# A two-layer bottleneck network: the last stage's held rows moved between the last tile's products, and VectorE's order written out in three places

## The chip, the cores and the metric

The kernel runs on one core of a Trainium2 chip. A core has TensorE (PE, matrix products, results in PSUM), VectorE (DVE), ScalarE (ACT), GpSimd (POOL) and SyncE (SP, which here only issues DMAs). The engines run side by side and wait for one another through semaphores. The metric is the device time of one execution in microseconds (us), as the median of several runs; fewer is better.

## The reference

Two layers in a row, each a residual bottleneck on 64 images of 1024 channels and 14 x 14 pixels, all in 32-bit floats:

```python
out = relu(bn(conv1x1(x, w1) + b1))        # 1024 -> 256 channels
out = relu(bn(conv3x3(out, w2) + b2))      # 256 -> 256
out = bn(conv1x1(out, w3) + b3)            # 256 -> 1024
x   = relu(x + softplus(residual_scale) * out)
```

`bn` takes its mean and variance over all images and pixels of the batch, so a layer's last normalization can only be applied when the statistics of all pixels are known. The change touches what follows that point in the second layer.

## The kernel before, in words

Channels lie on the 128 partitions. A *tile* t (0 to 31) is two images, PX = 392 pixels; its 1024 channels are CS = 8 *rows* of 128 x 392. The 256 channels after the second convolution stay in SBUF as `y`, in MS = 2 slots.

The statistics of the second layer's last convolution come from a Gram matrix of `y` (`gram`). VectorE transposes `y` piece by piece from a copy called `home` (L1309) into small `zt` tiles, of which there are six in a ring; TensorE multiplies each with itself into the bank `ap`. In between, TensorE makes the products of tile 0, which ACT saves as `z` (eight rows), and ENDED = 3 products of the last tile 31, which ACT saves as `held`. The closure `beside` hangs other work on given steps of that loop: four weight sums (L148), and at step `total - 4` the four sums of `y` that the first pair of tiles needs (`pair_sums`, `column_sums`, L501 to L504).

Then `final`, the last stage. The third convolution of tiles 1 to 30 is done in 15 *pairs* of tiles, with seven block products in place of eight (a Strassen-like scheme), so each pair needs four sums of `y` (L501 to L504, tiles `ct`) and sums of weights (`ws`). A *unit* (`Conv3Pair`) is one pair and two of its rows, q and q + 4; there are 60 units. A unit has seven products, p1 to p7, of 128 x 392 each, in the PSUM banks `cy`, `cx` and `cp` (two of each). Around them stand:

- ACT copies scaled banks to `cu` (after p1, p6 and p7), so that the bank can be written again;
- VectorE adds scaled banks to the rows of x (`add`, L536, after p2, p3, p4 and p5);
- GpSimd adds `cu` to the rows of x (L559 after p7, L667 after p3);
- ACT applies the last ReLU in place to three of the unit's four rows (`end`), VectorE to the fourth (L676, in `go_out`), and SP issues the unit's two stores (L679).

`stream` sets the order of the products: a unit's p3 and p4 are done within the following unit (`last`), and the first two units begin together. `stream` yields once per product; `final` counts these yields in k and hangs tile 0's rows on them. The eight rows of tile 0 are completed by `residual`: a VectorE instruction that adds the scaled `z` row to the x row (L1816), and an ACT ReLU that the caller issues later. `go_out` is called once more than two units are open. The rows 0 to 2 of tile 31 are completed from `held` in the last pair, one for each of its first three units, by `residual(...)()`. `ending` then makes the products of tile 31's rows 3 to 7 (the last in two halves), completes them and stores the tile in pieces (L1846); rows 0 and 1 are stored together.

What sets the order: all products (L167) and all ACT calls through `act` (L342) are given to their engines in the order of the program. VectorE's, GpSimd's and SP's instructions are not, unless `tc.keep_in_program_order` is called on them: then an instruction is put behind the one that was traced before it on its engine. All others the planner of the language sorts at compile time, by its own estimate of when each is ready and by their place in the program; it may bring an instruction far forward. `run(ins)` pins an instruction only while the list `pinned` has an entry. `go_out`'s L676 is always pinned, the stores never are.

The tiles of x come by DMA into six buffers; tile 31's load is issued while the pair 27 and 28 is worked on.

Of the kernel before, what the change touches and what calls it, by code (L numbers as in the profile page):

```python
# [12 lines left out]
ALU = mybir.AluOpType  # L13
# [5 lines left out]
CS = C // P  # L19
# [54 lines left out]
def bottlenecks(ctx: ExitStack, tc: tile.TileContext, x, w1s, w2s, w3s, pars, out):  # L74
# [1736 lines left out]
    def residual(xt, o, ps, aff, here=slice(0, PX)):  # L1811


        scale, shift = aff
        v = xt[:, o, here]
        nc.vector.scalar_tensor_tensor(v, ps, scale[:, o : o + 1], v, ALU.mult, ALU.add)  # L1816
        return partial(act, v, v, AF.Relu, bias=shift[:, o : o + 1])
# [13 lines left out]

    def ending(psum, xt, w3, aff):

        for o in range(CS):
            parts = 2 if o + 1 == CS else 1
            for i in range(parts):
                here = slice(i * PX // parts, (i + 1) * PX // parts)
                if o >= ENDED:
                    ps = psum.tile(PX // parts)
                    for s in range(MS):  # L1840
                        matmul(ps, w3[:, s, o, :], two(T - 1, s)[:, here], start=s == 0, stop=s == MS - 1)
                    residual(xt, o, ps, aff, here)()
                a = o - 1 if o % 2 and o + 1 < CS else o
                if o % 2 or o + 2 == CS:
                    queue = nc.scalar if o + 1 == CS and i + 1 == parts else nc.sync
                    queue.dma_start(  # L1846
                        out=out[T - 1][:, a * PX + here.start : o * PX + here.stop],
                        in_=xt[:, o, here] if a == o else xt[:, a : o + 1].rearrange("p s f -> p (s f)"),
                    )

# [4 lines left out]
    def final(psum, pool, sums_pool, xpool, xs, z, held, summed, a, w3, aff):  # L1855
# [4 lines left out]
        def pairs():  # L1860
            for t in range(1, T - 1, 2):
                ys, sums = summed.pop(0) if summed else pair_sums(sums_pool, t)
                for q in range(CS // 2):
                    units.append(Conv3Pair(psum, pool, xs[t : t + 2], q, PX, ys, sums, w3, aff, out[t : t + 2]))
                    yield units[-1]

                    while len(units) > 2:
                        units.pop(0).go_out()
                    if t == T - 3 and q < ENDED:
                        residual(xs[T - 1], q, held[:, q], aff)()  # L1870
                    if q == 1:

                        for i in range(len(xs), min(t + len(xpool), T)):
                            xs.append(load_x(xpool[i % len(xpool)], 1, i))

        relus = [residual(xs[0], o, z[:, o], aff) for o in range(HELD)]
        for k, _ in enumerate(stream(pairs(), (T // 2 - 1) * CS // 2, together=True), 1):
            if k % 2 == 0 and k // 2 <= CS - HELD:
                o = HELD + k // 2 - 1
                relus.append(residual(xs[0], o, z[:, o], aff))  # L1880
            if k % 2 == 0 and relus:
                relus.pop(0)()
                if not relus:
                    nc.gpsimd.dma_start(out=out[0], in_=xs[0].rearrange("p s f -> p (s f)"))
        for unit in units:
            unit.go_out()
        ending(psum, xs[T - 1], a, aff)

# [323 lines left out]
    for b in range(2):  # L2212
# [9 lines left out]
        with tc.tile_pool(name=f"last_{b}", bufs=1, **({"reuse_waits": "tile"} if b == 0 else {})) as one, tc.tile_pool(  # L2222
# [12 lines left out]
            with ExitStack() as scope:  # L2235
# [10 lines left out]
                with tc.tile_pool(name=f"gram_{b}", bufs=1) as pool:  # L2246
# [11 lines left out]
                    else:  # L2258
# [4 lines left out]
                        beside = {total - 14 + 2 * i: partial(next, summed) for i in range(4)}  # L2263
                        beside[total - 4] = lambda: first_sums.append(pair_sums(sums_pool, 1))
                        grams = gram(psum, pool, homes, z, own, aff, minus_c, w3, beside)
# [76 lines left out]
```

## Time and profile before

| | |
|---|---|
| median of 3 runs | 1891.18 us (1890.45 to 1892.38) |
| profiled execution | 1890.67 us |
| its span, first to last instruction | 1888.9 us |
| TensorE busy | 1867.8 us, 99% |
| VectorE busy | 1573.1 us, 83% |
| ScalarE busy | 1111.2 us, 59% |
| GpSimd busy | 742.1 us, 39% |
| first product of the last stage starts | 1592.13 us |
| last product of the last stage starts | 1882.82 us |

How to read the rows that follow. A row of the timeline reads: start in us, duration in us from the first start to the last end of the merged instructions, engine, line, operation, output<-inputs, shape, count, and in square brackets how long the engine had been idle and what ended that. Buffer numbers are left out of names: `cy` is either of two banks. One product of 128 x 392 is two matmul instructions (x2). PEld is the loading of weights, which overlaps PE; DVEq, SPq and ACTq are the engines' sequencers, which issue DMAs and wait on semaphores. Ends of matmuls are modelled, so distances between starts are used here. A row of the chain of waits reads: start, duration, what. A row of a table by stretch reads: from:to, length, busy time of each engine with its count, granted TensorE clock, share of the DMA engines, GB/s.

### The profile page before, as it was taken

To read this page: it belongs to the slowest core of one execution; us is meant where nothing else is said; L and a number is where in the kernel's file an instruction comes from. 1 tells how busy PE (TensorE), PEld (TensorE's weight loads), DVE (VectorE), ACT (ScalarE), POOL (GpSimd) and SP (SyncE) were. 2 spreads that over 40 slices of the span, in tenths; PEclk is the share of its full clock that TensorE was granted. 3 is DMA by queue.
4 is the path that set the end of the run, shared out by engine and by line. 5 is a ranking of instruction groups with operands and counts; after the bars stand their busy time and mean duration, and the time that the engine had idled before them with its cause. 6 is when DMAs were issued, how large, how long until landed. Compare 5 with 4: busy or idle time off the path is not lost. (4 is left out here: it accounts for less than half of the span.)

```text
span 1888.9 us, 28626 instructions
## 1 busy us (share of the span) xinstructions
PE 1867.8 (99%) x9728; PEld 1555.5 (82%) x9728; DVE 1573.1 (83%) x2494; ACT 1111.2 (59%) x2329; POOL 742.1 (39%) x763
## 2 busy tenths in 40 slices
PE   9999999999999999999999999999999999999998
PEld 5555557999998998899999999999999986555554
DVE  5787867999998776778788788799999986888886
ACT  2222214677777665555555555457777694666665
POOL 0111100121205655377776776311121151666665
PEclk9999999999999999999999999999999999999999
DMA  7777644797865556778788887468788465999997
GB/s 288 269 253 271 217 182 137 204 218 216 207 201 163 183 175 213 252 270 321 269 281 299 296 297 278 193 184 223 212 208 221 141 175 224 343 338 334 334 347 281
DMA packets 246609, 458.87 MB, mean 243 GB/s; under 512 B 41456, under 2 KB 212992, under 8 KB 233280
## 3 DMA queue, kind: packets, MB, share of 16 engines
q1 hardware_dynamic: 208288, 375.30, 58.8%
q0 software_dynamic: 31328, 29.18, 7.9%
q10 hardware_dynamic: 6848, 52.57, 6.9%
q8 instruction: 77, 1.26, 0.3%
q14 instruction: 68, 0.56, 0.1%
HBM read 289.44 MB, written 141.03 MB: 228 GB/s over the span
## 5 line engine op out<-in xcount | busy, mean ns | idle before, releaser
L167 PE MATMUL columns<-v,ub 128*128 128x224 f32 (+1 forms) x1536 | 303.5, 339 | 1.4 <-ACT columns L342 0.8
L342 ACT ACTIVATE x<-x,shift 128x392 f32<-128x392 f32 x453 | 260.3, 613 | 71.7 <-DVE x L536 31.4
L167 PEld LDWEIGHTS columns<-v,ub 128*128 128x128 f32 x1536 | 268.6, 188 | 8.4 <-ACT columns L342 1.5
L342 ACT ACTIVATE cu<-cy,scale 128x196 f32<-128x196 f32 (+1 forms) x360 | 175.5, 499 | 163.0 <-PE cy L167 155.5
L167 PE MATMUL ay<-at,ws 128*128 128x196 f32 (+1 forms) x760 | 191.6, 383 | 0.4 <-ACT au L342 0.2
L667 POOL TENSOR_TENSOR x<-x,cu 128x392 f32<-128x392 f32 x120 | 125.7, 1048 | 111.5 <-DVE x L536 109.4
L167 PEld LDWEIGHTS ay<-at,ws 128*128 128x128 f32 x760 | 134.8, 190 | 35.7 <-issue 0.9
L536 DVE SCALAR_TENSOR_TENSOR x<-cp,scale,x 128x196 f32<-128x196 f32 (+1 forms) x240 | 124.4, 518 | 45.6 <-PE cp L167 44.2
L342 ACT ACTIVATE au<-ay 128x196 f32<-128x196 f32 (+1 forms) x139 | 53.5, 385 | 169.8 <-PE ay L167 159.8
L167 PE MATMUL l<-diffs,ub 128*128 128x224 f32 (+1 forms) x768 | 149.7, 337 | 0.4 <-DVE diffs L803 0.3
L167 PE MATMUL m<-sums,ua 128*128 128x224 f32 (+1 forms) x752 | 146.0, 336 | 1.2 <-issue 0.6
L167 PEld LDWEIGHTS l<-diffs,ub 128*128 128x128 f32 x768 | 134.6, 189 | 1.8 <-DVE diffs L803 1.1
L167 PEld LDWEIGHTS m<-sums,ua 128*128 128x128 f32 x752 | 131.4, 189 | 2.7 <-issue 0.9
L1104 POOL DMA_DIRECT2D y<-f x24 | 32.1, 1636 | 257.5 <-DVE f L1003 257.5
L167 PE MATMUL cx<-y,w 128*128 128x196 f32 (+1 forms) x404 | 124.7, 395 | 0.0
L559 POOL TENSOR_TENSOR x<-x,cu 128x196 f32<-128x196 f32 (+1 forms) x120 | 104.3, 869 | 45.7 <-ACT cu L342 27.3
L167 PE MATMUL cy<-y,w 128*128 128x196 f32 (+1 forms) x372 | 115.6, 398 | 1.7 <-ACT y L342 0.9
L342 ACT ACTIVATE y<-y,shift,scale 128x320 f32<-128x320 f32 (+9 forms) x105 | 110.2, 1074 | 7.1 <-DVE shift L2082 6.4
L564 POOL TENSOR_TENSOR x<-x,cu 128x392 f32<-128x392 f32 x60 | 80.4, 1340 | 84.8 <-DVE x L536 82.0
L214 POOL DMA_DIRECT2D u<-y x48 | 26.0, 543 | 211.3 <-ACT y L342 210.5
L963 ACT ACTIVATE columns<-m 128x448 f32<-128x448 f32 (+1 forms) x144 | 70.8, 492 | 56.1 <-PE m L167 49.1
L1931 POOL TENSOR_SCALAR y<-y,scale 128x392 f32<-128x392 f32 x57 | 92.3, 1620 | 28.5 <-DVE scale L2283 28.5
(331 smaller groups left out, 4510.7 us busy)
## 6 DMA issues: line engine op xcount, KB each, us to landing
ub<-u SPq DMA_DIRECT2D x92, 768.0 KB, 5.5
x<-in_x SPq DMA_DIRECT2D x35, 1568.0 KB, 8.3
x<-mid SPq DMA_DIRECT2D x32, 1568.0 KB, 7.5
out<-x SPq DMA_DIRECT2D x123, 392.0 KB, 6.9
mid<-x ACTq DMA_DIRECT2D x30, 1568.0 KB, 9.1
x<-in_x SPq DMA_DIRECT2D x108, 392.0 KB, 7.8
ua<-u SPq DMA_DIRECT2D x92, 256.0 KB, 3.1
z<-kept SPq DMA_DIRECT2D x60, 392.0 KB, 2.9
```

The lines of the kernel that those rows point to most:

```text
L167: tc.keep_in_program_order(nc.tensor.matmul(*args, **kw))
L214: nc.gpsimd.dma_start(out=us[b][i][:, s, o], in_=u)
L342: tc.keep_in_program_order(nc.scalar.activation(*args, **kw))
L536: run(nc.vector.scalar_tensor_tensor(v, bank, self.scale[:, o : o + 1], v, ALU.mult, ALU.add))
L559: run(nc.gpsimd.tensor_add(self.part(1, 1), self.part(1, 1), u3))
L564: run(nc.gpsimd.tensor_add(v, v, self.u12))
L667: nc.gpsimd.tensor_add(v, v, self.u12[:, i * self.n : (i + 1) * self.n])
L963: copy(v, m, AF.Copy)
L1104: nc.gpsimd.dma_start(out=out_rows[3][:, o], in_=fa[:, o, :full], accum_op=ALU.add)
L1931: run(nc.gpsimd.tensor_scalar(z, z, scale[:, o : o + 1], None, ALU.mult))
```

## The change

Five edits in the second layer's last part.

1. `residual` issues its VectorE instruction through `run`, so it is pinned where `pinned` is set.
2. In the last pair of `final`, the three calls of `residual` on the held rows are gone, and `go_out` is called once more than one unit is open (before: two).
3. In `final`, VectorE and GpSimd instructions that go through `run` are pinned up to the 14th product. Rows 0 to 4 of tile 0 are still begun ahead of the products; rows 5, 6 and 7 are begun at k = 5, 8 and 11 (before: 2, 4 and 6).
4. `ending` is rewritten: after the product of row 3, 4 and 5 each, held row 0, 1 and 2 is completed; all of its VectorE instructions are pinned. Rows 0 and 1 are stored after row 4's product, rows 2 and 3 and rows 4 and 5 after row 5's.
5. The four sums for the first pair are pinned at step `total - 4` of the Gram loop.

```diff
@@ residual
-        nc.vector.scalar_tensor_tensor(v, ps, scale[:, o : o + 1], v, ALU.mult, ALU.add)
+        run(nc.vector.scalar_tensor_tensor(v, ps, scale[:, o : o + 1], v, ALU.mult, ALU.add))
         return partial(act, v, v, AF.Relu, bias=shift[:, o : o + 1])
@@ ending
-    def ending(psum, xt, w3, aff):
-
-        for o in range(CS):
-            parts = 2 if o + 1 == CS else 1
-            for i in range(parts):
-                here = slice(i * PX // parts, (i + 1) * PX // parts)
-                if o >= ENDED:
-                    ps = psum.tile(PX // parts)
-                    for s in range(MS):
-                        matmul(ps, w3[:, s, o, :], two(T - 1, s)[:, here], start=s == 0, stop=s == MS - 1)
-                    residual(xt, o, ps, aff, here)()
-                a = o - 1 if o % 2 and o + 1 < CS else o
-                if o % 2 or o + 2 == CS:
-                    queue = nc.scalar if o + 1 == CS and i + 1 == parts else nc.sync
-                    queue.dma_start(
-                        out=out[T - 1][:, a * PX + here.start : o * PX + here.stop],
-                        in_=xt[:, o, here] if a == o else xt[:, a : o + 1].rearrange("p s f -> p (s f)"),
-                    )
+    def ending(psum, xt, held, w3, aff):
+
+        def store(a, e, queue=nc.sync):
+            queue.dma_start(out=out[T - 1][:, a:e], in_=xt.rearrange("p s f -> p (s f)")[:, a:e])
+
+        def product(o, i=0, parts=1):
+            here = slice(i * PX // parts, (i + 1) * PX // parts)
+            ps = psum.tile(PX // parts)
+            for s in range(MS):
+                matmul(ps, w3[:, s, o, :], two(T - 1, s)[:, here], start=s == 0, stop=s == MS - 1)
+            residual(xt, o, ps, aff, here)()
+
+        pinned.append(True)
+        for o in range(ENDED, CS - 1):
+            product(o)
+            if o < 2 * ENDED:
+                residual(xt, o - ENDED, held[:, o - ENDED], aff)()
+            for a, e, by in (0, 2, 4), (2, 4, 5), (4, 6, 5), (6, 7, 6):
+                if by == o:
+                    store(a * PX, e * PX)
+        for i in range(2):
+            product(CS - 1, i, 2)
+            a = (CS - 1) * PX + i * PX // 2
+            store(a, a + PX // 2, (nc.sync, nc.scalar)[i])
+        pinned.clear()
@@ final
-                    while len(units) > 2:
+                    while len(units) > 1 + (t < T - 3):
                         units.pop(0).go_out()
-                    if t == T - 3 and q < ENDED:
-                        residual(xs[T - 1], q, held[:, q], aff)()
                     if q == 1:
 
                         for i in range(len(xs), min(t + len(xpool), T)):
                             xs.append(load_x(xpool[i % len(xpool)], 1, i))
 
+        pinned.append(True)
         relus = [residual(xs[0], o, z[:, o], aff) for o in range(HELD)]
         for k, _ in enumerate(stream(pairs(), (T // 2 - 1) * CS // 2, together=True), 1):
-            if k % 2 == 0 and k // 2 <= CS - HELD:
-                o = HELD + k // 2 - 1
+            if k in (5, 8, 11):
+                o = HELD + (k - 5) // 3
                 relus.append(residual(xs[0], o, z[:, o], aff))
+            if k == 14:
+                pinned.clear()
             if k % 2 == 0 and relus:
                 relus.pop(0)()
                 if not relus:
                     nc.gpsimd.dma_start(out=out[0], in_=xs[0].rearrange("p s f -> p (s f)"))
         for unit in units:
             unit.go_out()
-        ending(psum, xs[T - 1], a, aff)
+        ending(psum, xs[T - 1], held, a, aff)
@@ bottlenecks, beside the Gram loop
-                        beside[total - 4] = lambda: first_sums.append(pair_sums(sums_pool, 1))
+
+                        def sums_now():
+                            pinned.append(True)
+                            first_sums.append(pair_sums(sums_pool, 1))
+                            pinned.clear()
+
+                        beside[total - 4] = sums_now
```

## The prediction

> **What bounds the kernel now.** I read the page first, then the busy times by stretch of the last stage, then PE's timeline for starts that come late, then the other engines' timelines at those places.
>
> ```profile
> PE 1867.8 (99%) x9728; PEld 1555.5 (82%) x9728; DVE 1573.1 (83%) x2494; ACT 1111.2 (59%) x2329; POOL 742.1 (39%) x763
> 1621.00:1858.00 237.00, 237.00 (x712) 134.08 (x711) 198.47 (x305) 161.20 (x305) 164.20 (x153) 1.00 0.95 338
> 1858.00:1877.00 19.00, 16.27 (x49) 8.65 (x48) 12.86 (x21) 12.12 (x24) 9.99 (x10) 1.00 0.67 243
> 1877.00:1889.00 12.00, 6.65 (x25) 4.12 (x23) 5.89 (x11) 5.07 (x9) 2.24 (x3) 0.87 0.72 263
> ```
>
> TensorE is the bound: 237.00 of 237.00 us busy in the middle of the last stage, at a granted clock of 1.00. So only places where PE starts late, and what follows its last product, can give time. In the stretch up to 1877 it is 2.73 us short (19.00 - 16.27); after that the work drains into DMA.
>
> ```profile
> 1859.78 0.82 PE L167 MATMUL cy<-ct,w 128*128 128x392 f32 x2
> 1863.31 0.93 PE L167 MATMUL cy<-ct,ws 128*128 128x392 f32 x2 [2.71 <-ACT cu L342]
> 1861.18 2.02 DVE L1816 SCALAR_TENSOR_TENSOR x<-held,scale,x 128x392 f32<-128x392 f32 x3
> 1862.16 0.62 ACT L342 ACTIVATE x<-x,shift 128x392 f32<-128x392 f32 x1 [2.88 <-DVE x L1816]
> 1862.68 0.57 ACT L342 ACTIVATE cu<-cy,scale 128x392 f32<-128x392 f32 x1
> 1865.55 1.32 PE cy L167 x4
> 1872.13 1.32 PE cy L167 x4
> ```
>
> The last two rows (from the chain of waits) are 10 products apart: 0.658 us a product. The rows above show the largest stall: the three held rows' VectorE work stands together at 1861.18. ACT, whose order is fixed, has the first held row's ReLU ahead of a `cu` copy, waits 2.88 us for it, and PE needs the copy.
>
> **The change part by part.**
>
> *Held rows out of the last pair (edit 2).* The step 1859.78 to 1863.31 is 3.53, less 0.66 is 2.87; and the product that starts at 1863.31 takes 0.93 where the one before it takes 0.82, 0.10 more. Together 2.97 us. With the ReLU gone, ACT's copy has nothing to wait for but its bank. What is late next? Unit 58 instead gets a second L676 (0.9 us, by the rows of the ending below); VectorE has three held instructions fewer there (2.02 us), so it is not later than now. The ReLUs of held rows 1 and 2 also leave the pair. I take -2.97; the other end is 0, if another wait fills the place.
>
> *First products (edit 3).*
>
> ```profile
> 1591.98 4.38 DVE L1816 SCALAR_TENSOR_TENSOR x<-z,scale,x 128x392 f32<-128x392 f32 x8
> 1595.42 1.48 PE L167 MATMUL cy<-ct,ws 128*128 128x392 f32 x4
> 1596.82 0.61 DVE L536 SCALAR_TENSOR_TENSOR x<-cp,scale,x 128x392 f32<-128x392 f32 x1
> 1597.48 0.93 PE L167 MATMUL cp<-y,ws 128*128 128x392 f32 x2 [0.59 <-DVE x L536]
> 1598.02 1.01 POOL L559 TENSOR_TENSOR x<-x,cu 128x392 f32<-128x392 f32 x1
> 1596.28 1.25 ACT L342 ACTIVATE cu<-cy,scale 128x392 f32<-128x392 f32 x2
> 1599.06 2.80 ACT L342 ACTIVATE x<-x,shift 128x392 f32<-128x392 f32 x5 [1.03 <-POOL x L559]
> 1602.38 0.93 PE L167 MATMUL cy<-ct,w 128*128 128x392 f32 x2
> ```
>
> The planner has brought all eight rows of tile 0 ahead of the first adds. With 4.38/8 = 0.55 each, five pinned rows end at about 1594.7, the add from `cx` at 1595.2, row 5 at 1595.7. The `cp` add needs the product that ends where the two `cy` products (x4) start, 1595.42; it is then next in the queue and ends at about 1596.4 instead of 1597.43. PE's `cp` product can then start at 1595.42 + 1.32 = 1596.74, 0.74 earlier. But the gain does not all stay: at 1602.38 PE waits for ACT, which did five ReLUs in a row after waiting for GpSimd's L559. L559 needs the add and the later of the two `cu` copies, which ACT ends at 1597.53, so it can start at about 1597.57, 0.45 earlier, not 1.07. ACT's five ReLUs and PE's product at 1602.38 move by that. I take -0.46. Ends: -1.13, all that PE loses here (0.74 and 0.11 at 1597.48, 0.28 at 1602.38), and +0.5, below among the rivals.
>
> *The first pair's sums (edit 5).*
>
> ```profile
> 1558.98 0.55 DVE L501 TENSOR_TENSOR ct<-y 128x392 f32<-128x392 f32 x1
> 1560.88 0.55 DVE L504 TENSOR_TENSOR ct<-y,ct 128x392 f32<-128x392 f32 x1
> 1561.36 1.29 DVE L1309 STREAM_TRANSPOSE zt<-home 128x512 f32<-128x512 f32 x2
> 1564.94 3.98 DVE L1309 STREAM_TRANSPOSE zt<-home 128x512 f32<-128x512 f32 x7
> 1560.74 0.75 PE L167 MATMUL ap<-zt 128*64 128x193 f32 x8
> 1562.11 6.80 PE L167 MATMUL ap<-zt 128*64 128x193 f32 x96 [0.62 <-DVE zt L1309]
> 1575.88 2.96 PE L167 MATMUL ap<-zt 128*64 128x193 f32 x40
> 1558.70 2.18 DMA home<-y
> ```
>
> Five sums (one of them for the second pair) stand from 1558.98 to 1561.36 in front of a transpose, and PE waits for that transpose. PE's 96 matmuls take 6.80, so eight take 0.57: after 1560.74 it would go on at 1561.31, not 1562.11: 0.80 lost. Step `total - 4` puts the four sums between the eighth and ninth of the last eleven transposes, after the first four of the row of seven. The last three transposes then come 4 x 0.48 = 1.9 us later, at about 1570; PE needs them at 1575.88, some 6 us of cover. Without that cover the cost would be 1.9. The transpose needs data, though: the chain of waits names a move into `home` that ends at 1560.88. By that, only 1561.36 - 1560.88 = 0.48 can be won. But the transpose starts 0.48 after L504 did, the very spacing of the sums, so I read VectorE's queue as what held it, and take -0.80. Ends: -0.80 and 0.
>
> *The ending (edits 2 and 4), in the times of before.*
>
> ```profile
> 1867.70 0.57 SPq L1846 DMA_DIRECT2D out<-x  x1
> 1877.64 1.82 DVE L676 TENSOR_SCALAR x<-x,shift 128x392 f32<-128x392 f32 x2
> 1879.28 0.62 ACT L342 ACTIVATE x<-x,shift 128x392 f32<-128x392 f32 x1 [0.47 <-POOL x L667]
> 1878.40 0.53 SPq L679 DMA_DIRECT2D out<-x  x1
> 1884.14 0.46 ACT L342 ACTIVATE x<-x,shift 128x196 f32<-128x196 f32 x1
> GB/s 368 13 0 0 0 0 0 155 393 381 142 0 0 0 29 372 355 351 381 376 364 385 372 376 368 385 393 368 393 393 401 381 345 339 322 44 0 0 0 0
> ```
>
> PE's products are the same. VectorE now has three L676 here (the first two shown), then two, and gains three held instructions of 0.54: from 1877.64 + 1.82 = 1879.46 it runs row 3, held 0, row 4, held 1, row 5, held 2 until about 1882.7; the last three are bound by PE as now. ACT runs seven ReLUs of some 0.54 from 1879.28 + 0.62 = 1879.9, and the last one, now at 1884.14, comes about 0.1 later.
>
> DMA decides more. The rate row (0.375 us a slice, from 1874) is full from about 1879.5 to 1887.4: the store issued at 1878.40 begins to move 1.1 later, and with those behind it 7 x 392 KB (two rows of 128 x 392 floats each) go out in 7.9 us, 1.1 each at some 365 GB/s. The change moves rows 0 and 1 (392 KB) from 1867.70 into this queue, past SP's other stores, and takes one store of unit 58 out of it, to before 1876. The amount is equal. But three stores are done at 1879.5 + 3.3 = 1882.8, and rows 0 and 1 cannot go before held row 1's ReLU, about 1882.3; their data begin 1.1 later, at 1883.4. From there four times 1.1 ends at 1887.8, not 1887.4. I take +0.4. Ends: -0.2 (ACT's last store, issued at 1884.6, alone decides) and +1.1 (392 KB that find no gap).
>
> The Trainium skill (DMA: Bandwidth & Descriptors, section "Anatomy of one DMA") fits a transfer as about 2.0 us plus bytes at 436 GB/s. By that, an estimate from its figures, 392 KB would take 0.92 in the queue instead of 1.10 and this term would be near -0.2. The slices here top out near 400 GB/s and average some 365, so the trace does not agree; the sum keeps the rows.
>
> *What comes along: the second pair's sums.*
>
> ```profile
> 1606.44 0.82 PE L167 MATMUL cp<-y,ws 128*128 128x392 f32 x2
> 1608.61 1.45 DVE L502 TENSOR_TENSOR ct<-ct,y 128x392 f32<-128x392 f32 x1
> 1617.18 0.82 PE L167 MATMUL cy<-ct,w 128*128 128x392 f32 x2
> 1654.71 1.32 PE cy L167 x4
> 1841.51 1.32 PE cy L167 x4
> ```
>
> Ten pairs later in the stage take 186.80, 18.68 each, against 28 x 0.658 = 18.42: 0.26 lost per pair, at its sums. At the second pair's sums PE loses more: 15 products from 1606.44 to 1617.18 take 10.74, not 9.87: 0.87. VectorE's sum takes 1.45 there, with GpSimd behind its usual place. Engines that come 0.46 earlier may relieve part of it; the planner decides anew. I take -0.2, between -0.6 (as a later pair) and +0.6.
>
> **The sum.** -2.97 - 0.46 - 0.80 + 0.4 - 0.2 = -4.0. The profiled execution took 1890.67 (span 1888.9 and 1.8 around it), so 1886.7; the median is 0.51 above it: 1887.2.
>
> **Rivals.**
>
> ```profile
> L1816 DVE SCALAR_TENSOR_TENSOR x<-held,scale,x x3: 614/615/940, 1861.2 to 1862.6; 128x392 f32<-128x392 f32 x3
> 1860.69 1.01 POOL L667 TENSOR_TENSOR x<-x,cu 128x392 f32<-128x392 f32 x1 [0.32 <-DVE x L536]
> ```
>
> *The tail or the start takes its full price.* The tail at +1.1, or the start at +0.5: rows 6 and 7 of tile 0 now stand in the time of GpSimd's adds, and the first held row, begun at 1861.18 while an add of GpSimd ran, took 0.94 against 0.61 for the other two. If two such rows each wait out most of a 1.01 us add, `cp` adds come late and the start loses what it gained. Against it: ACT, not VectorE, is the bound there once the `cp` add is early, which leaves VectorE slack. The Trainium skill (SBUF — State Buffer, section "Who interferes with whom") says that a VectorE instruction with two SBUF inputs and a GpSimd instruction reading SBUF exclude each other, so that one waits in full. By that rule this price is due wherever the two meet; the 0.94 agrees with it. With either price: -3.0 to -3.4, about 1888.1.
>
> *More comes along.* The second pair's sums fall to the usual 0.26, and the tail finds its gap: -5.0, 1886.2. For it: later pairs show that rate with the same order of instructions.
>
> *The stall stays under another name.* ACT's order is still fixed and the two L676 of unit 58 come at its start; if PE waits there for VectorE or the planner moves the stores into SP's way, edit 2 gives nothing: -1.0, about 1890.2. Against it: 2.02 us of VectorE's work leave the same place.
>
> *Slower.* The planner re-sorts the unpinned VectorE and GpSimd work of all pairs behind the new start. If every pair's sums met GpSimd as the second pair's do, each of 13 pairs would lose 0.61 more: +7.9 - 4.0 = +3.9, 1895.1. It decides from 0.31 us a pair on. Against it: ten pairs in a row return to the same 18.68, whatever happened at 1608.
>
> **How the numbers follow.** The forecast 0.46, tail or start in full 0.22, more comes along 0.18, the stall stays 0.06, slower 0.08. 0.2% (3.8 us) is about what a measurement of this kernel can tell from no change. The forecast's own range, 1886.4 to 1888.0, straddles that bound: 0.30 over it and 0.16 within. So faster 0.48, same 0.16 + 0.22 + 0.06 = 0.44, slower 0.08. The range 1885.2 to 1889.4 holds the first three cases and leaves out the last two and some edges, about 0.2.
>
> **What would show it.** Right: no PE idle of over 0.3 us in the last pair; held instructions between L1816's of `cy` and `cx` only, spaced 0.54; the first `cp` product of the stage 0.66 after its neighbour, and ACT still the releaser of a `cy` product some 5 us on; no PE idle before the last eleven transposes, sums between the eighth and ninth; DMA nearly full over the last 8 us, its data ending 0.4 us later behind the last product than now. Wrong: a new releaser of PE in units 57 to 60, more than 18.8 us a pair, or a DMA hole over 1 us before rows 0 and 1 go out.

## The result, and the profile after

The changed kernel takes 1886.76 us (median of 11 runs, 1886.01 to 1888.36), the kernel before 1891.87 us in the same comparison (11 runs, 1890.22 to 1892.77). The ratio is 0.9975, with a 95% interval of 0.9966 to 0.9984: faster by 0.25%, just over what this kernel's measurement can tell from no change. Predicted were 1887.2 us. The profiled execution took 1886.24 us, its span is 1884.5 us, 4.4 less than the 1888.9 of before.

The page of the changed kernel (busy time of the engines), and its busy times by stretch of the last stage; the columns are those of the prediction's first fence:

```profile
PE 1867.1 (99%) x9728; PEld 1556.6 (83%) x9728; DVE 1572.8 (83%) x2494; ACT 1111.7 (59%) x2329; POOL 744.6 (40%) x763
```

```profile
1618.00:1855.00 237.00, 237.00 (x712) 134.03 (x711) 198.54 (x305) 161.26 (x305) 164.72 (x153) 1.00 0.97 341
1855.00:1871.00 16.00, 15.98 (x49) 8.84 (x49) 11.24 (x19) 11.19 (x22) 9.84 (x10) 1.00 0.79 282
1871.00:1884.50 13.50, 7.04 (x26) 4.37 (x24) 7.29 (x13) 6.43 (x12) 2.63 (x3) 0.96 0.65 238
```

TensorE bounds the stage as before. The stretch before the ending, 2.73 us short in the kernel before, is now full (15.98 of 16.00). The last row is 1.5 us longer than before's (13.50 against 12.00, partly by where it was cut), with VectorE busy for 7.29 instead of 5.89: the held rows have come there.

The places that the prediction names, in the timelines of the changed kernel, from the Gram products to the last pair:

```profile
1564.13 1.31 DVE L1309 STREAM_TRANSPOSE zt<-home 128x512 f32<-128x512 f32 x2 [0.87 <-PE ap L167]
1565.36 1.00 DVE L501 TENSOR_TENSOR ct<-y 128x392 f32<-128x392 f32 x2
...
1567.23 0.56 DVE L504 TENSOR_TENSOR ct<-y,ct 128x392 f32<-128x392 f32 x1
1567.71 1.63 DVE L1309 STREAM_TRANSPOSE zt<-home 128x512 f32<-128x512 f32 x3
...
1552.73 14.67 PE L167 MATMUL ap<-zt 128*64 128x129 f32 x212
...
1593.91 1.48 PE L167 MATMUL cy<-ct,ws 128*128 128x392 f32 x4
1595.23 0.82 PE L167 MATMUL cp<-y,ws 128*128 128x392 f32 x2
...
1600.40 0.93 PE L167 MATMUL cy<-ct,w 128*128 128x392 f32 x2
...
1597.20 2.67 ACT L342 ACTIVATE x<-x,shift 128x392 f32<-128x392 f32 x5 [0.68 <-POOL x L559]
...
1857.14 0.82 PE L167 MATMUL cy<-ct,w 128*128 128x392 f32 x2
1857.80 0.82 PE L167 MATMUL cy<-ct,ws 128*128 128x392 f32 x2
```

All sums stand behind the eighth of the last eleven transposes, and PE goes through 212 Gram matmuls without a gap. The stage's first `cp` product starts 1.32 behind the two `cy` products (x4), with no wait. ACT still has its five ReLUs in a row behind GpSimd's L559, so a wait of 0.28 us is left at the `cy` product of 1600.40. The two `cy` products that were 3.53 us apart at the held rows are 0.66 apart.

The ending: VectorE, ACT and SP by time, the DMA rate (0.41 us a slice from 1868.2), and SP's own waits over the last pair (what it waited for, us in total, times, the longest):

```profile
1872.03 1.83 DVE L676 TENSOR_SCALAR x<-x,shift 128x392 f32<-128x392 f32 x2
1873.78 0.61 DVE L1816 SCALAR_TENSOR_TENSOR x<-cy,scale,x 128x392 f32<-128x392 f32 x1
1874.31 0.61 DVE L1816 SCALAR_TENSOR_TENSOR x<-held,scale,x 128x392 f32<-128x392 f32 x1
1868.36 1.63 ACT L342 ACTIVATE x<-x,shift 128x392 f32<-128x392 f32 x3
1866.00 1.20 SPq L679 DMA_DIRECT2D out<-x  x2
1872.83 0.53 SPq L679 DMA_DIRECT2D out<-x  x1
```

```profile
GB/s 377 381 296 0 0 0 0 0 0 0 0 0 0 0 262 358 381 373 369 381 354 381 373 385 393 408 423 370 369 377 383 421 319 385 333 83 0 0 0 0
```

```profile
SPq L679 <- DVE x L676: 13.7, 4, 5.6
```

VectorE's order is as written. But SP issues nothing between 1867.2 and 1872.83, and DMA moves nothing for eleven slices. Unit 59's store of tile 30 was ready when ACT's three ReLUs ended, at 1870.0. It stands in SP's queue behind unit 59's store of tile 29, which waits for L676 at 1872.03. Then seven stores of 392 KB and the three pieces of rows 6 and 7 (392 KB together) go out in one row. In the kernel before, ACT's three ReLUs of unit 59 and SP's next store read:

```profile
1873.97 1.63 ACT L342 ACTIVATE x<-x,shift 128x392 f32<-128x392 f32 x3
1875.63 0.53 SPq L679 DMA_DIRECT2D out<-x  x1
```

There tile 30's store goes out 0.03 us behind its ReLUs, 2.77 ahead of the next one (1878.40), and is no part of the last row. That row has six stores of 392 KB and the three pieces: one store less.

**Where the time went.** Steps between the same products of PE, worked out from their start times in each profile: 18 Gram matmuls around the gap; from the stage's first product pair to the `cy` product that waits for ACT; the 15 products at the second pair's sums; ten later pairs; the two `cy` products at the held rows; from there to the last product; from its start to the span's end. The kernels of the experiments stand below.

| kernel | Gram | start | second pair | ten pairs | held rows | rest | tail |
|---|---|---|---|---|---|---|---|
| before | 2.07 | 10.26 | 10.75 | 186.80 | 3.53 | 19.52 | 6.07 |
| changed | 1.21 | 9.78 | 10.05 | 186.84 | 0.66 | 19.41 | 7.25 |
| e8_before | 2.16 | 10.25 | 10.75 | 186.83 | 3.53 | 21.21 | 6.07 |
| e8_after | 1.20 | 9.78 | 10.05 | 186.84 | 0.66 | 19.42 | 7.25 |
| e1_sums | 1.21 | 10.26 | 10.05 | 186.81 | 3.52 | 19.52 | 6.07 |
| e2_start | 2.13 | 9.77 | 10.75 | 186.81 | 3.53 | 21.02 | 6.07 |
| e3_end | 2.15 | 10.26 | 10.05 | 186.83 | 0.66 | 19.42 | 7.25 |
| e4_inplace | 2.15 | 10.26 | 10.05 | 186.81 | 3.52 | 22.30 | 6.07 |
| e4_relus | 1.95 | 10.25 | 10.04 | 186.81 | 0.66 | 20.17 | 7.12 |
| e5_swap | 1.20 | 9.78 | 10.75 | 186.81 | 0.66 | 19.41 | 6.46 |
| e6_port | 1.21 | 10.37 | 10.97 | 184.33 | 0.66 | 19.41 | 6.34 |
| e7_all | 1.20 | 10.38 | 10.87 | 184.33 | 0.66 | 20.28 | 5.30 |
| e9_best | 1.21 | 9.58 | 9.88 | 184.33 | 0.66 | 20.03 | 5.45 |
| e10_late | 1.20 | 9.59 | 9.88 | 184.33 | 0.66 | 19.42 | 5.60 |

Changed less before: -0.86 - 0.48 - 0.70 + 0.04 - 2.87 - 0.11 + 1.18 = -3.80. Another -0.58 lies ahead of every changed place (the `cy` product with which tile 0 begins starts at 1510.40, not 1510.98; over the fourteen profiles it starts between 1509.90 and 1511.73). The rest, below 0.1, lies between the steps.

### The profile page after: what moved, and what is told of

Its sections match the earlier page's. It is cut to its first block, busy times and chain, and to the rows that moved or that the text cites. A ratio compares the mean times of both kernels' runs of the same rounds, so it can differ in the third digit from the quotient of the medians.

```text
span 1884.5 us, 28626 instructions
## 1 busy us (share of the span) xinstructions
PE 1867.1 (99%) x9728; PEld 1556.6 (83%) x9728; DVE 1572.8 (83%) x2494; ACT 1111.7 (59%) x2329; POOL 744.6 (40%) x763
## 5 line engine op out<-in xcount | busy, mean ns | idle before, releaser
L559 POOL TENSOR_TENSOR x<-x,cu 128x196 f32<-128x196 f32 (+1 forms) x120 | 104.9, 874 | 46.6 <-ACT cu L342 18.6
```

The lines of the kernel that those rows point to most:

```text
L559: run(nc.gpsimd.tensor_add(self.part(1, 1), self.part(1, 1), u3))
```

## The experiments

The expectations count the tail to the last byte, some 1.1 us ahead of the span's end that the table uses: their 5.0 is the table's 6.07, their 6.10 its 7.25.

### The three places one by one

`e1_sums`, edit 5 alone:

```diff
-                        beside[total - 4] = lambda: first_sums.append(pair_sums(sums_pool, 1))
+                        def sums_now():
+                            pinned.append(True)
+                            first_sums.append(pair_sums(sums_pool, 1))
+                            pinned.clear()
...
+                        beside[total - 4] = sums_now
```

> The kernel before with edit 5 alone (the first pair's sums fixed behind the eighth of the last eleven transposes). Theory (VectorE's queue held the transpose): the row of 96 Gram products and the row of 40 join without an idle stretch, 0.80 to 0.86 us won, and nothing else in the last stage moves: 10.25 us from the stage's first product of a pair to the cy product that waits for ACT, 10.74 us over the 15 products at the second pair's sums, 3.53 us at the held rows, 5.0 us from the last product to the last byte. Rival 1 (the move into home held it): 0.48 won. Rival 2 (moving the sums is what relieved the second pair's sums, one of the five being theirs): the 10.74 falls to about 10.05 here.

Measured: 1888.34 us against 1890.93. The Gram step falls by 0.86, so VectorE's queue held the transpose. The second pair fell to 10.05 too, as the second rival had it. The next two kernels tell whether that comes from the sums.

`e2_start`, edits 1 and 3 alone (`run(...)` around `residual`'s instruction, and the loop of `final`):

```diff
+        pinned.append(True)
         relus = [residual(xs[0], o, z[:, o], aff) for o in range(HELD)]
...
-            if k % 2 == 0 and k // 2 <= CS - HELD:
-                o = HELD + k // 2 - 1
+            if k in (5, 8, 11):
+                o = HELD + (k - 5) // 3
...
+            if k == 14:
+                pinned.clear()
```

> The kernel before with edits 1 and 3 alone (VectorE's order fixed at the stage's first products). Theory: 10.25 us from the first product of the stage to the cy product that waits for ACT becomes 9.78 (0.47 won); the Gram gap of 0.80, the 3.53 at the held rows and the tail of 5.0 stay. For the second pair's sums, theory A: what is late there is set by the start, so 10.74 falls to about 10.05 with this edit alone, 1.16 won in all. Theory B: it comes from elsewhere, and 10.74 stays, 0.47 won in all.

Measured: 1891.64 us against 1890.93. The start won 0.49, and the second pair stayed at 10.75: theory B. Yet the time is no better, for 1.50 us were lost in "rest", behind a stall that this edit doesn't touch. The busy times by stretch show why; the third column from the right is the clock that PE was granted:

```profile
1859.01:1862.42 3.41, 1.06 (x4) 0.29 (x2) 2.94 (x5) 0.80 (x2) 1.84 (x2) 1.00 1.05 370
1862.42:1865.84 3.42, 3.07 (x5) 1.80 (x6) 0.29 (x2) 1.66 (x4) 0.00 (x0) 0.50 0.45 155
```

From 1862.42 on, just ahead of the end of the stall at the held rows, PE's clock was half for 3.4 us.

`e3_end`, edits 1, 2 and 4 alone (the new `ending`, and in the pairs):

```diff
-                    while len(units) > 2:
+                    while len(units) > 1 + (t < T - 3):
                         units.pop(0).go_out()
-                    if t == T - 3 and q < ENDED:
-                        residual(xs[T - 1], q, held[:, q], aff)()
```

> The kernel before with edits 1, 2 and 4 alone (held rows out of the last pair, completed in the ending). Theory: 3.53 us at the held rows becomes 0.66 to 0.7 and no other idle of over 0.3 us appears in the last pair, 2.97 won; the tail from the last product to the last byte grows from 5.0 to 6.1, because the second store of unit 59 stands in SP's queue behind its first, which waits for VectorE's L676: 1.9 us won in all. Rival for the tail (rows 0 and 1 going out late are its whole cause, 0.4): 5.4. The start (10.25) and the second pair's sums (10.74) stay.

Measured: 1888.00 us against 1890.93. The held step becomes 0.66 (2.87 less, and 0.10 more in "rest"), and the tail grows by 1.18, not by the rival's 0.4. The second pair came out at 10.05, with every instruction of every engine there in the order of before. So that 0.70 is none of the edits'.

### Two things that change from one execution to the next

Both kernels unchanged, profiled again:

> The kernel before, unchanged, profiled again. Theory (two things in its profile are a matter of the execution and not of the program: at the second pair's sums a VectorE sum and a GpSimd add become ready within 0.02 us of each other and either may win the port; after the stall at the held rows PE's granted clock either stays 1.0 or falls to 0.5 for 2 to 3 us): the 15 products at the second pair's sums take 10.74 or about 10.05 us with nothing between; the step at the held rows is 3.53 us again, with or without 1.3 to 1.6 us more behind it. Rival (they belong to the program): 10.74 again and nothing more behind the stall.

> The changed kernel, unchanged, profiled again. Theory as in the run before it: 10.05 or 10.74 us over the 15 products at the second pair's sums (10.05 in its first profile), PE's granted clock at 1.0 through the last pair since no stall is left there. Rival (the change relieves the second pair's sums): 10.05 again. The sum of the terms otherwise within 0.3 us of its first profile, from the Gram products to the last byte.

Measured: 1893.31 and 1886.46 us. The kernel before has the 10.75 again, and this time loses 1.69 us behind its stall:

```profile
1864.20:1867.40 3.20, 3.18 (x6) 1.84 (x7) 0.63 (x1) 2.12 (x4) 0.10 (x1) 0.62 0.65 224
```

Of the five profiles that have the stall of some 2.7 us, two kept a clock of 1.00 behind it (before and e1_sums) and three did not (e2_start, e4_inplace, e8_before). The clock thus belongs to the execution. In the three, the half clock lasts 3.41 us each (from 1862.42, 1862.59 and 1864.97), and PE was busy for 0.71 to 1.06 us of the 3.41 us ahead of it. The Trainium skill (TensorE: Matmul & The Clock Gate, section "What's actually happening") describes it: a monitor counts PE's activity in free-running windows of about 3.4 us, and an idle window halves the clock. The trace agrees as to the half (0.50), the length (3.41) and the chance of it. That a stall of 2.7 us, shorter than such a window, can be enough, it shows beyond the page.

The second pair is the same kind of thing. Rows of three kernels, VectorE's sum L502 and GpSimd's adds; first the kernel before, then e1_sums, then e5_swap (below):

```profile
1607.65 1.98 POOL L667 TENSOR_TENSOR x<-x,cu 128x392 f32<-128x392 f32 x2
```

```profile
1606.99 0.57 DVE L502 TENSOR_TENSOR ct<-ct,y 128x392 f32<-128x392 f32 x1
1606.04 3.39 POOL L667 TENSOR_TENSOR x<-x,cu 128x392 f32<-128x392 f32 x3
```

```profile
1606.46 1.46 DVE L502 TENSOR_TENSOR ct<-ct,y 128x392 f32<-128x392 f32 x1
1605.51 1.99 POOL L667 TENSOR_TENSOR x<-x,cu 128x392 f32<-128x392 f32 x2
```

GpSimd's second add and VectorE's sum start within 0.02 to 0.03 us of each other: 1608.63 and 1608.61 in the kernel before. Where GpSimd gets the port, the sum takes 1.45 (quoted in the prediction) and PE loses 0.70. Where VectorE gets it, the sum takes 0.57 and GpSimd's add 1.42, which costs PE nothing. The order of before lost in before, e2_start and e8_before, and won in e1_sums, e3_end, e4_inplace and e4_relus. The changed kernel won in its two profiles, and e5_swap, which differs only in its last stores, lost. The recorded starts don't tell them apart: in all ten profiles the sum's stands 0.018 to 0.029 us ahead of the add's, whichever of the two is held up. What breaks the tie stays open.

### What the stall at the held rows was

`e4_inplace`, the kernel before with the three VectorE instructions in written order:

```diff
                     if t == T - 3 and q < ENDED:
-                        residual(xs[T - 1], q, held[:, q], aff)()
+                        pinned.append(True), residual(xs[T - 1], q, held[:, q], aff)(), pinned.clear()
```

> The kernel before with the held rows left in the last pair, ReLUs and stores as they are, but their VectorE instructions in written order (one at its place, the second and third behind the next two L676). Theory A, the reading of the prediction (three held rows standing together are what delays ACT): the wait of 2.88 us of ACT for the first of them shrinks by the 1.1 us of the other two at least, and PE's step of 3.53 us to 2.4 or less. Theory B (ACT's ReLU of the first held row, ahead of the copy that PE needs, waits for the first held row alone, whose tile has been loaded late and which stands behind two adds): ACT still waits 2.7 to 2.9 us, PE's step stays 3.4 to 3.6 us, and the other two cost PE waits of their own where they now stand.

Measured: 1892.35 us against 1890.93. The step stays 3.52:

```profile
1861.05 0.62 ACT L342 ACTIVATE x<-x,shift 128x392 f32<-128x392 f32 x1 [2.87 <-DVE x L1816]
1861.58 0.57 ACT L342 ACTIVATE cu<-cy,scale 128x392 f32<-128x392 f32 x1
```

Theory B: the three instructions in one place were not the cause. ACT waits for the first alone, which stands behind two adds, and that place is the same. The other two now cost PE 0.34 and 0.73 where they stand, by their ReLUs ahead of a copy, beside 1.70 at half clock.

`e4_relus`, the same instructions left in the pair, only their ReLUs taken out of it:

```diff
-                        residual(xs[T - 1], q, held[:, q], aff)()
+                        held_relus.append(residual(xs[T - 1], q, held[:, q], aff))
...
+        for relu in held_relus:
+            relu()
```

> The kernel before with the three held rows' VectorE instructions left in the last pair and only their ReLUs taken out of it (issued after the last pair's stores). Theory (ACT's ReLU, ahead of the copy that PE needs, is the whole stall; VectorE has room for 2 us more in the last pair): PE's step of 3.53 us becomes 0.66 to 0.7 and no other idle over 0.3 us comes in the pair, 2.97 won. Rival (VectorE's 2 us of held work is itself what PE pays for): a stall of 1 us or more of PE stays somewhere in the last pair, with VectorE as its releaser or that of ACT.

Measured: 1887.82 us against 1892.72. The step is 0.66: ACT's ReLU ahead of the copy was the whole of that stall. But the rival has a share: "rest" is 0.76 above the changed kernel's. PE waits for VectorE at one `cp` product; the held instructions met GpSimd's adds ahead of a `cp` add (1.38 and 1.06 instead of 0.61):

```profile
1862.74 1.38 DVE L1816 SCALAR_TENSOR_TENSOR x<-held,scale,x 128x392 f32<-128x392 f32 x1
...
1865.12 1.06 DVE L1816 SCALAR_TENSOR_TENSOR x<-held,scale,x 128x392 f32<-128x392 f32 x1
1867.31 0.93 PE L167 MATMUL cp<-y,ws 128*128 128x392 f32 x2 [0.49 <-DVE x L536]
```

### What the tail was

`e5_swap`, the changed kernel with the last two units' stores in the other order:

```diff
-        def go_out(self):
+        def go_out(self, order=(0, 1)):
...
-            for i in range(2):
+            for i in order:
...
         for unit in units:
-            unit.go_out()
+            unit.go_out((1, 0))
```

> The changed kernel with the two stores of unit 59, and of unit 60, issued second tile first; no other instruction moves. From the start of the last product to the last byte the changed kernel takes 6.10 us. Theory 1 (SP's queue: unit 59's second store, ready at its ReLUs, stood behind the first, which waits for L676): SP issues the store of tile 30 about 2 us earlier, DMA's hole before the ending shrinks by 1.1 us, and 6.10 becomes 5.0 to 5.4. Theory 2 (rows 0 and 1, completed late, are what fills the queue): 6.0 to 6.2 stays.

Measured: 1885.99 us. SP issues tile 30's store 7.20 us ahead of the last product, where in the changed kernel it stands 3.76 ahead (1873.45), second behind the first issue after the hole. DMA's eleven empty slices become six, and the tail is 6.46 instead of 7.25, in the expectation's count 5.3: theory 1. Two kernels that leave these stores to the planner agree. In e6_port (below) it puts tile 30's store first again, at 1869.14, and the tail is 6.34. In e4_relus, whose rows 0 and 1 are stored in the ending, the last row of stores begins as far ahead of the last product as in the kernel before (4.4 us) and also has one store more; the tail is 7.12 there. So one store more in that row costs about the 1.1 us that it takes.

```profile
1870.52 0.53 SPq L679 DMA_DIRECT2D out<-x  x1
```

```profile
GB/s 380 376 376 376 43 0 0 0 67 384 380 173 0 0 0 90 376 388 149 157 361 392 373 380 392 423 392 408 376 376 392 392 353 376 320 159 0 0 0 0
```

The 0.39 that is left over the kernel before is not due to rows 0 and 1 here: the rate falls to 149 and 157 ahead of unit 60's stores (the first issued at 1874.81, 1.52 behind the store ahead of it), and is full from there on. In e6_port the 0.27 that is left goes with a dip ahead of rows 0 and 1, as the prediction had it.

### A faster version

In the changed kernel a steady pair loses 0.26 us to the same port:

```profile
1646.58 0.55 DVE L503 TENSOR_TENSOR ct<-y 128x392 f32<-128x392 f32 x1
1647.05 1.38 DVE L501 TENSOR_TENSOR ct<-y 128x392 f32<-128x392 f32 x1
1648.35 0.61 DVE L536 SCALAR_TENSOR_TENSOR x<-cp,scale,x 128x392 f32<-128x392 f32 x1
1646.58 1.42 POOL L559 TENSOR_TENSOR x<-x,cu 128x392 f32<-128x392 f32 x1
```

L501 waits out GpSimd's L559, and the `cp` add behind it comes late. `e6_port` makes one sum a unit, behind the `cy` add (`pinned` stays set to the end of the pairs, all four `ct` doubled):

```diff
+        def after4(self):
+            self.add(1, 0, self.y)
+            self.then()
...
+        def sums_ahead(t):
+            ys = [[two(t + i, s) for i in range(2)] for s in range(MS)]
+            t1, t2, t3, t4 = sums = column_sums(sums_pool, ys, PX, range(4), made=True)
+            summed.append((ys, sums))
+            yield run(nc.vector.tensor_sub(t3, ys[1][1], ys[0][1]))
...
+                ahead = sums_ahead(t + 2) if t < T - 3 else iter(())
...
+                    units[-1].then = partial(next, ahead, None)
```

> The changed kernel with the sums of each following pair made one a unit, behind the cy add of VectorE, in four doubled buffers, VectorE's order fixed throughout. Theory (the loss of 0.26 us a pair, and the 0.70 more or less at the second pair's sums, come from sums that meet a GpSimd add on the shared port: 1.37 us instead of 0.55, in front of the cp add): a pair takes 18.42 to 18.50 us instead of 18.68, 2.4 to 3.4 us won over the stage, and every sum takes under 1.0 us. Rival (the pairs' first products cost PE the 0.26 by themselves, or a sum waits for GpSimd at the new place just as long and delays the cx add): 18.6 us or more a pair.

Measured: 1884.45 us. Ten pairs take 184.33, 18.43 each: PE is full there. The sums still meet GpSimd (0.95 us), but at a place where VectorE has 0.54 us to spare in each unit. The first pair is worse, which the expectation left out (start and second pair 1.5 us above the changed kernel's together): PE waits 0.60 for VectorE at a `cp` product beside tile 0's rows, 0.22 at one behind a sum of 1.80 (every sum was expected under 1.0), and 0.72 for ACT at a later `cy` product.

```profile
1645.68 0.95 DVE L1878 TENSOR_TENSOR ct<-y 128x392 f32<-128x392 f32 x1
1649.09 0.63 DVE L536 SCALAR_TENSOR_TENSOR x<-cp,scale,x 128x392 f32<-128x392 f32 x1 [0.54 <-PE cp L167]
...
1602.73 1.80 DVE L1877 TENSOR_TENSOR ct<-ct,y 128x392 f32<-128x392 f32 x1
1602.47 0.59 POOL L1906 DMA_DIRECT2D out<-x  x1 [0.64 <-ACT x L342]
1603.07 1.02 POOL L672 TENSOR_TENSOR x<-x,cu 128x392 f32<-128x392 f32 x1
```

`e7_all` adds the start's and the ending's edits:

```diff
-            if k % 2 == 0 and relus:
+            if k in (2, 4, 6, 8, 9, 12, 14, 16):
...
+                    if t == T - 3 and q < ENDED:
+                        units[-1].then = partial(residual, xs[T - 1], q, held[:, q], aff)
...
+            if k == 417:
+                units.pop(0).go_out((1, 0))
+            if k == 412:
+                nc.sync.dma_start(out=out[T - 1][:, : 2 * PX], in_=xs[T - 1][:, :2].rearrange("p s f -> p (s f)"))
```

> As the one before, and three more edits: tile 0's fifth ReLU one step earlier (ahead of the three ReLUs that wait for GpSimd), the held rows' VectorE instructions and ReLUs behind the adds and the ReLUs of units 57 to 59, their store and unit 59's earlier, second tile first. Theory: the 0.28 us at the cy product of the stage's start goes; PE has no idle over 0.3 us in the last pair, since each held ReLU stands behind the unit's own ones and not ahead of a copy that is due; DMA has no hole of over 1 us before the last product, and from the start of the last product to the last byte 4.3 to 4.8 us instead of 6.10. With the pairs, 4.5 to 5.3 us under the changed kernel: 1881 to 1882. Rival (a held row in the last pair costs PE wherever it stands, as it did before): a stall of 0.5 us or more in units 58 to 60; rival for the tail (the last store's own way is the bound): over 5.2 us.

Measured: 1883.53 us, 1.5 more than expected. The tail is 5.30 (4.11 in the expectation's count), shorter than expected. The 0.28 at the start's `cy` product is gone, but the start stays at 10.38, since PE waits 0.61 for VectorE at the `cp` product ahead of it, as in e6_port. The rival holds in the pair: 0.87 lost in "rest", some 0.5 of it behind four ReLUs in a row ahead of a copy:

```profile
1867.09 2.15 ACT L342 ACTIVATE x<-x,shift 128x392 f32<-128x392 f32 x4
1869.77 0.93 PE L167 MATMUL cy<-ct,w 128*128 128x392 f32 x2 [0.28 <-ACT cu L342]
```

`e9_best` puts each held ReLU into ACT's idle time behind the first copy of a later unit, and the second pair's sums into the Gram stage:

```diff
-                            first_sums.append(pair_sums(sums_pool, 1))
+                            first_sums.extend(pair_sums(sums_pool, t) for t in (1, 3))
...
+            if k in (407, 414, 419):
+                held_relus.pop(0)()
```

> The one-sum-a-unit version with all eight sums of the first two pairs made in the Gram stage (behind the eighth of the last eleven transposes), tile 0's fifth ReLU a step earlier, the held rows' VectorE instructions behind the cy adds of units 57 to 59 and their ReLUs in ACT's idle time behind a first cu copy, their store and unit 59's earlier, second tile first. Theory: no loss at the start beyond what the changed kernel has (its 9.78 us from the first product to the cy product that waits for ACT, or 0.28 less), 18.43 us a pair, no stall over 0.3 us in units 58 to 60 (what cost PE 0.86 us in the version before were four ReLUs in a row ahead of a copy), and 4.3 to 4.8 us from the start of the last product to the last byte: 5.0 to 6.0 us under the changed kernel's 1886.2, thus 1880.3 to 1881.3, ratio to the kernel before about 0.994 to 0.995. Rival 1 (three more sums in the Gram stage push the last transposes past PE's need): an idle stretch of 0.5 us or more before the last row of Gram products. Rival 2 (VectorE's held rows, which meet a GpSimd add at their place, cost PE by themselves): 0.4 us or more lost in units 58 to 60.

Measured: 1881.48 us (median of 5, 1880.87 to 1883.29) against 1890.45; ratio 0.9954, interval 0.9940 to 0.9967. Start, pairs and Gram step are as expected, and the three more sums cost nothing. The median lies just over the expected range, for a gap is left in unit 58: "rest" is 0.62 above the changed kernel's, the sign that rival 2 named.

```profile
1857.09 0.63 DVE L1821 SCALAR_TENSOR_TENSOR x<-held,scale,x 128x392 f32<-128x392 f32 x1 [0.83 <-ACT x L342]
1858.84 0.93 PE L167 MATMUL cp<-y,ws 128*128 128x392 f32 x2 [0.35 <-DVE x L536]
```

But its length is not that of a meeting on the port (0.63, not 0.94): VectorE waited 0.83 to start. The row names ACT, on which this instruction doesn't depend; what it needs is tile 31. The load of tile 31 reads (in the timeline, and in the list of DMAs, where the last figure is the time to landing):

```profile
1848.45 0.33 SPq L117 DMA_DIRECT2D x<-mid  x1
x<-mid SPq DMA_DIRECT2D x1, 1568.0 KB, 8.6
```

It landed at 1857.01, and VectorE's wait for that load's semaphore ended at 1857.05. So this gap is the load's, not the port's. `e10_late` puts the held rows one unit later, the third into the ending:

```diff
-                    if t == T - 3 and q < ENDED:
+                    if t == T - 3 and 0 < q < ENDED:
...
-            if k in (407, 414, 419):
+            if k in (414, 419):
...
+            if o == ENDED:
+                residual(xt, 2, held[:, 2], aff)()
```

> As the version before, but the held rows one unit later: two of them behind the cy adds of units 58 and 59, the third in the ending, the store of rows 0 and 1 after unit 59's stores. Theory (in the version before VectorE waited 0.83 us at unit 57 for tile 31, whose load is issued some 8.6 us ahead of it, and PE paid 0.62 for the cx and cp adds behind it): the gap of PE in unit 58 goes, no product of the last pair starts over 0.3 us late, the tail stays within 0.3 us of the version before, and the time comes 0.3 to 0.7 us under its 1881.5. Rival (a held row that meets a GpSimd add at this place costs PE whatever the load does): a gap of 0.3 us or more of PE moves to unit 59 or 60.

Measured: 1881.48 us (median of 5, 1881.09 to 1882.44) against 1891.23; ratio 0.9950, interval 0.9936 to 0.9963, so faster than the changed kernel, whose interval begins at 0.9966. The gap is gone ("rest" 19.42), though a held row meets GpSimd for 0.94 a unit later; the load landed at 1854.53, five us ahead of it. The expected 0.3 to 0.7 us don't show in the median, which is that of e9_best; between the two profiles these steps differ by 0.46. Of the wait of 0.68 ahead of ACT's ReLUs at the start, 0.16 is left:

```profile
1597.14 2.16 ACT L342 ACTIVATE x<-x,shift 128x392 f32<-128x392 f32 x4 [0.16 <-POOL x L559]
```

## Why the prediction came out right, and where it didn't

- *Held rows out of the last pair, -2.97:* -2.87 and -0.10, alone (e3_end) as in the whole. The sum's price is right, the reading only in part. That ACT has the first held row's ReLU ahead of a copy was the cause (e4_relus). That the three instructions stood together was not (e4_inplace). And "VectorE has three held instructions fewer" was worth 0.76 of its own in e4_relus, which no row of before showed, since there PE stood still while they ran. What the step left out: behind that stall the clock can halve, for 1.5 to 1.7 us more. With a clock of 1.00 in the profile of before, its rows could not tell it.
- *First products, -0.46:* -0.48, by the chain that was named (the add, L559, ACT's five ReLUs). The 0.28 at the `cy` product stayed, as said.
- *The first pair's sums, -0.80:* -0.86. VectorE's queue held the transpose, and the rival reading by the chain of waits (0.48) falls.
- *The ending, +0.4:* +1.18, beyond the end given as +1.1. This is the term that failed, and the step in it is "the amount is equal". "Takes one store of unit 58 out of it" is right, and rows 0 and 1 come in for it. But the step never asked in which order unit 59's stores would stand. In the kernel before the planner had put tile 30's store first, and it was gone before the last row of stores began; in the changed kernel it stands behind the one that waits for L676. So that row has one store of 392 KB more, about 1.1 us. Putting tile 30's stores of units 59 and 60 first gives 0.79 back (e5_swap); how much of the 0.4 foreseen for rows 0 and 1 is real stays open (they follow without a gap in e5_swap, behind a short one in e6_port). The text even named "a DMA hole over 1 us before rows 0 and 1 go out" as the sign of being wrong, and the hole is 4.5 us. The fit that the prediction names from the Trainium skill (DMA: Bandwidth & Descriptors, section "Anatomy of one DMA") is given there for DMAs that GpSimd issues. These are SP's, and the sum rightly kept the rows.
- *The second pair's sums, -0.2, end -0.6:* -0.70 between the two profiles, and not the change's. "The planner decides anew" was wrong: the order there is unchanged, and the port's tie fell the other way. That it moved the way that was forecast is luck.
- *The sum, -4.0:* the profiles differ by 4.4. The ending's 0.8 too little was made up by the tie's 0.5 and by 0.58 that the profiles differ by ahead of every edit. So the three large terms of the start, the sums and the held rows are right by their mechanism, but that the total came within half a microsecond is luck. The median fell by 5.1. A clock that halves in part of the executions of before, and in none of the profiles without the stall, goes in that direction. The mean clock of whole runs fits it (0.998 in 8 of 20 runs of before in the experiments, never under 0.999 in the changed kernel's 11), but it doesn't tell where in the run the clock fell, so how often it halves there stays open.
- *The rivals:* the tail took its full price; the start did not, though row 6 of tile 0 met GpSimd as that rival described (0.84). No later pair became slower (ten pairs 186.84), so the slower one's mechanism did not come about.

## What to carry to other kernels

On an engine that works in order, look at what stands *behind* an instruction with a late operand, and the queue that issues DMAs is such an engine: here a store that was ready at 1870.0 stood behind one that could go only at 1872.83, and one store more was left for the end. Where two engines share a port, don't move an operation to where its neighbour is idle but to where its own engine has slack, so that either order costs nothing (e6_port's sums of 0.95 in front of 0.54 of idle time). Before a difference between two profiles is explained by an edit, look whether the same step differs between two executions of one program.

## What the runs showed of the hardware

- A stall of PE of some 2.7 us is in itself a risk: in three of five profiles PE's granted clock fell to half about its end (0.50 over 3.41 us each), for 1.5 to 1.7 us more.
- VectorE's sum and GpSimd's add, which start within 0.02 to 0.03 us of each other, are served in either order by the execution: 0.57 or 1.46 us for the same sum. The Trainium skill (SBUF — State Buffer, section "Who interferes with whom") says that the order of issue, not the operation, decides which of the two blocks. The same two operations do come out either way here; the order of issue can't be read off, since the sum's recorded start is the earlier one in both outcomes.
- In one case (e6_port), a sum whose start is recorded while GpSimd issued a DMA (0.59 us) ended 0.44 us after GpSimd's next add had: 1.80 us in all, against 0.95 in the steady pairs. That the DMA issue itself held it up is argued from this one case.
